# Routed attention in a six-layer decoder: keys and values by blocks of one head, with scatter and gather

## The chip, the cores and the metric

The kernel runs on one core of one Trainium2 chip. The metric is the time of one execution on the device in microseconds (us); of several runs the median is given. All data are fp32, apart from small helpers.

## The reference

The program is a decoder of six sublayers on x of shape 8 x 256 x 512 (2048 tokens, 16 tiles of 128), each followed by an added residual and a layer norm: differential attention, a long convolution, a mixture of 8 experts, self attention, cross attention, and at last the routed attention that the change is about:

```
gating = softmax(x @ W_gate.T)                # 16 heads
idx    = argmax(gating)                       # one head per token
q, k, v = split(x @ W_qkv.T, 3)               # 512 columns each, 16 heads of 32
k_shared = k of head idx of the token         # one key of 32 for each token
v_shared = v of head idx, times max(gating)
att = softmax(causal(q_h @ k_shared.T / sqrt(32)))
y_h = att @ v_shared                          # for all 16 heads of q
x   = layernorm(x + y)
```

Every token has queries for all 16 heads, but only one key and one value of 32 numbers: those of the head that its gate chose. Of the 1024 columns of k and v, 64 are used for a token.

## The kernel before

One core does the sublayers one after the other. Two of them matter here.

**Cross attention** (`cross_attention`, L1548) goes over four groups of four tiles. For each group it turns x (`transpose`, L161), makes queries, keys and values by seven products instead of eight (`seven_products`, L1517: PE makes a product `ps` in PSUM, VectorE adds it on, L1537), and pushes two batches into a small pipeline of scores (`ps_x`), products (`po_x`) and output (`ps_o`, then the residual L1595 and the layer norm, whose reciprocal root runs on GpSimd, L139 and L140). Its instructions are ordered by the compiler's list scheduler, which may move an instruction ahead of others that are not ready. PSUM has four buffers with tag "mm", shared by the products and the transposes.

**Routed attention** (`routed_attention`, L1642) uses the common loop `causal_attention` (L1097). Here the order on PE, VectorE, ScalarE and GpSimd is the order in which the Python code emits the instructions. There are 32 units: four groups of two batches of four units. A unit u does `maxima` (scores `ps_q`, copied by ScalarE at L1160 to `rows`, masked by GpSimd at L1162, reduced by VectorE to `neg` at L1171), `products` of unit u-6 (`ps_pv` by L1257 and L1267, reciprocal L1275, product L1281), and `weights` of unit u-5 (scores again in `ps_k`, L1214; exponential on ScalarE, L1231; mask and a sum on GpSimd, L1232 and L1242). `ps_q` and `ps_k` share one PSUM tile of four banks.

Between these, `fill` and `need` (L1306, L1328) put in the group's other PE work in small steps. Each piece of work has a cost in us and a slot by which it is due; `pressure` (L1341) works out how much must go into each unit. Steps are in the list `queue`; pieces given with `at(..., "fill", ...)` come when nothing else has been begun. `prepare` (L1646) makes the pieces of a group: four turned tiles (`turned_group`, L197), the gate (`gates`, L1656: `ps_g`, then a softmax and the first maximum on VectorE), four `feature_block`s of queries (L1404, `ps_f`), and for each of four tiles two `token_block`s (L1414, `ps_t`): the keys of all 16 heads (512 columns) and the values of all 16 heads. From each of these 128 x 512 products VectorE picks the token's own head:

```
def chosen(dst, ps, by):                                   # L1673
    sel = ps * (one-hot of the head, broadcast over 32)    # L1676
    dst = sum over the 16 heads of sel                     # L1682
```

The keys are repeated four times (`k4`, L1687), turned (`keys_turned`, `pt_k`, L1692) and stored as `kT`. `finish` (L1726) turns the outputs back (`ps_y`), adds the residual into a `row` buffer (`add_norm_later`, L208; three buffers, each held until the norm in the next unit) and stores the tile.

The routing of tokens into blocks of one expert, which the mixture of experts already does (`router`, L669; `blocks`, L902), scatters rows of x to the DRAM tensor `xs` by indirect DMA on GpSimd, reads blocks of 128 rows of one expert back with SyncE's queue, reads the block's expert number into a register of PE (`values_load`, L915), and uses it to address the weights.

Of the kernel before, what the change touches and what calls it, by code (L numbers as in the profile page):

```python
# [23 lines left out]
P = 128  # L24
# [21 lines left out]
NE = (PH * 2 * P - E * (P - 1) - 1) // P + 1  # L46


@with_exitstack
def decoder_kernel(ctx: ExitStack, tc: tile.TileContext, a: dict, out: bass.AP):  # L50
# [43 lines left out]
    ctx_d = dram.tile([P, KB, B * S], F32, tag="ctx_d", name="ctx_d")  # L94

# [101 lines left out]
    def turned_group(work, pools, g):  # L197

        xT = []

        def step(ti):
            if ti == 0:
                xT.append(work.tile([P, KB, GT], F32, tag="xT", name="xT", bufs=1))
            turned(pools, xT[0][:, :, ti * P : (ti + 1) * P], x[g * TPG + ti])

        return xT, [(0, [(TR, lambda ti=ti: step(ti))]) for ti in range(TPG)]
# [405 lines left out]
    def experts(rt):  # L612
# [480 lines left out]
        return clear_slots, load_experts, load_gu_last, router, blocks, combine, wide  # L1093
# [3 lines left out]
    def causal_attention(name, prepare, finish, upb=KB, gather=None):  # L1097
# [18 lines left out]
        with ExitStack() as st:  # L1116
# [177 lines left out]
            def at(slots, place, f):  # L1294

                if place == "fill":
# [210 lines left out]
    def seven_tokens(work, xT):  # L1507

        (b11, b21), (b12, b22) = quadrants(xT)
        t = work.tile([P, 4, 2, S], F32, tag="ts", name="ts", bufs=1)  # L1510
        nc.vector.tensor_tensor(t[:, 0], b12, b11, ALU.subtract)
        nc.gpsimd.tensor_tensor(t[:, 2], b22, b12, ALU.subtract)
        nc.vector.tensor_tensor(t[:, 1], b22, t[:, 0], ALU.subtract)
        nc.vector.tensor_tensor(t[:, 3], b21, t[:, 1], ALU.subtract)
        return b11, b21, t[:, 1], t[:, 2], t[:, 3], t[:, 0], b22

    def seven_products(work, pools, weights, tokens, dst, token_major=False):  # L1517
# [15 lines left out]
        def part(name):  # L1533
            return work.tile([P, 2, S], F32, tag=name, name=name, bufs=1)

        p1, u2, u3 = part("p1"), part("u2"), part("u3")
# [3 lines left out]
        add(u2, product(2), p1)  # L1540
        add(u3, product(3), u2)
# [6 lines left out]
    def cross_attention(wq, wk, wv, wo):  # L1548
        scale = D**-0.5

        def batch(work, pools, ps_s, n, qT, kT, v, cx, ctxT):
# [34 lines left out]
            def out():  # L1586
                for i in range(2):
# [6 lines left out]
                    r = work.tile([P, D], F32, tag="row", name="res")  # L1594
# [6 lines left out]
        with ExitStack() as st:  # L1601
# [7 lines left out]
            for g in range(NG):  # L1609
# [14 lines left out]
                pipe.flush()  # L1624
                kT = work.tile([P, KB, GT], F32, tag="kT", name="kT", bufs=1)
                k = quadrants(kT)
                seven_products(work, pools, wk7, x7, lambda i, l: k[l][i])
                v = work.tile([P, TPG, D], F32, tag="v", name="v_x", bufs=1)
# [13 lines left out]
    def routed_attention(wqkv, wg):  # L1642

        idx = index_row(const, H1, "idx_h")

        def prepare(work, pools, g, at, here):  # L1646
# [5 lines left out]
            k4 = work.tile([P, TPG, 4, HD1], F32, tag="k4", name="k4")  # L1652
            ind = work.tile([P, TPG, H1], F32, tag="ind", name="ind")
            itop = work.tile([P, TPG, H1], F32, tag="itop", name="itop")

            def gates():  # L1656
                ps = pools.tile([P, TPG, H1], F32, tag="mm", name="ps_g")
                for ti in range(TPG):
                    project(
                        ps[:, ti, :],  # L1660
                        lambda k: xT[0][:, k, ti * P : (ti + 1) * P],
                        lambda k: wg[:, k, :],
                    )
                gate = work.tile([P, TPG, H1], F32, tag="gate", name="gate")
                nc.vector.tensor_copy(gate, ps)
                softmax_small(work, gate, H1)
                top = work.tile([P, TPG], F32, tag="top", name="top")
                first_max(work, gate, H1, idx, top, ind)
                nc.vector.tensor_tensor(
                    itop, ind, top.unsqueeze(2).broadcast_to([P, TPG, H1]), ALU.mult  # L1670
                )

            def chosen(dst, ps, by):  # L1673

                sel = work.tile([P, H1, HD1], F32, tag="sel", name="sel")
                nc.vector.tensor_tensor(  # L1676
                    sel,
                    ps.rearrange("p (h d) -> p h d", d=HD1),
                    by.unsqueeze(2).broadcast_to([P, H1, HD1]),
                    ALU.mult,  # L1680
                )
                nc.vector.tensor_reduce(dst, sel.rearrange("p h d -> p d h"), AX.X, ALU.add)  # L1682

            def key(ti, ps):
                k = k4[:, ti]
                chosen(k[:, 0, :], ps, ind[:, ti, :])
                nc.vector.tensor_copy(k[:, 1:4, :], k[:, 0:1, :].broadcast_to([P, 3, HD1]))  # L1687

            def keys_turned():
                pt = pools.tile([P, TPG, P], F32, tag="mm", name="pt_k")  # L1690
# [6 lines left out]
            xT, need = turned_group(work, pools, g)  # L1697
            need.append((0, [(0.8, gates)]))
            need.append((0, feature_block(pools, qT, xT, wqkv, 0, 0, HD1**-0.5)))
            for ti in range(TPG):  # L1700
                need.append(
                    (0, token_block(pools, xT, wqkv, D, ti, lambda ps, ti=ti: key(ti, ps)))
                )
            for c in range(1, 3):
                need.append((0, feature_block(pools, qT, xT, wqkv, 0, c, HD1**-0.5)))
            need.append((0, [(TR, keys_turned)]))
            for c in range(3, KB):
                need.append((c, feature_block(pools, qT, xT, wqkv, 0, c, HD1**-0.5)))
            for ti in range(TPG):
                need.append(  # L1710
                    (
                        5 + ti // 2 * (4 if g == NG - 1 else 2),
# [142 lines left out]
```

## Time and profile before

| what | us |
|---|---|
| median of 3 runs | 2199.62 (2196.56 to 2202.16) |
| the profiled execution | 2202.62 |
| its span, first to last instruction | 2200.8 |
| cross attention, its weights' sums included | from about 1502 to 1843 |
| routed attention | 1843 to 2200.8 |

The mean granted clock of TensorE in the profiled execution is 0.970. In the profile a row of a group gives the line, the engine, the operation, what it writes and reads, the shape and the count, then the busy time in us, the mean of one in ns, and the idle time of the engine before it with what ended it. Durations of PE matmuls overlap, because they are pipelined: the time that one costs in a full stream is the distance between the starts of two. PEld is the weight load, which runs beside the matmul before it; PEldq and PEq are steps of PE's sequencer.

### The profile page before, as it was taken

The numbers are of one execution on the slowest core, as the hardware profiler recorded it, in microseconds if no ns is written. First come the engines' busy times: TensorE is split into PE (matmuls) and PEld (weight loads), VectorE is DVE, ScalarE is ACT, GpSimd is POOL, SyncE is SP. The second block draws the span as 40 slices with busy tenths as digits, with TensorE's granted clock in tenths as the row PEclk, the third lists the DMA queues.
The fourth block names the chain that finished last, engine by engine and source line by source line (L and its number), as shares of the span: only waits on it lengthen the run. The fifth ranks groups of instructions, "written<-read, shape, count | busy, mean of one in ns | idle before, by whom it ended". The sixth has DMA issues, their size and how long they took to land. (4 is left out here: it accounts for less than half of the span.)

```text
span 2200.8 us, 35612 instructions
## 1 busy us (share of the span) xinstructions
PE 2053.4 (93%) x14904; PEld 1192.7 (54%) x14904; DVE 1272.1 (58%) x1923; ACT 598.9 (27%) x723; POOL 824.4 (37%) x918
## 2 busy tenths in 40 slices
PE   7989899879999999999959999999999999999995
PEld 4545555544453455555524444446877875445543
DVE  4676767758888964222235746466344343476777
ACT  4545545520010013111114333340110110333342
POOL 2566767737556723000033644343000000242343
PEclk9989999989999999999989999999999999999998
DMA  6899801335124144131140201002100100000000
GB/s 221 328 385 382 312 1 45 92 87 198 29 76 164 29 148 149 62 141 61 48 145 29 77 20 58 1 2 96 39 20 20 39 0 1 1 11 11 11 18 33
DMA packets 110032, 197.56 MB, mean 90 GB/s; under 512 B 7088, under 2 KB 30768, under 8 KB 109872
## 3 DMA queue, kind: packets, MB, share of 16 engines
q1 hardware_dynamic: 104752, 178.49, 23.4%
q0 software_dynamic: 5120, 16.78, 2.2%
q8 instruction: 120, 1.97, 0.4%
q14 instruction: 40, 0.33, 0.0%
HBM read 93.54 MB, written 112.20 MB: 93 GB/s over the span
## 5 line engine op out<-in xcount | busy, mean ns | idle before, releaser
L1275 DVE RECIPROCAL rsum<-ps_pv 128x256 f32<-128x256 f32 x128 | 224.4, 1753 | 238.1 <-PE ps_pv L1267 237.9
L171 PE MATMUL ps_y<-kv,wt 128*128 128x512 f32 x640 | 282.6, 600 | 4.4 <-POOL kv L519 3.8
L1231 ACT ACTIVATE pT<-ps_k 128x1536 f32<-128x1536 f32 x128 | 185.7, 1450 | 288.9 <-PE ps_k L1223 286.9
L1171 DVE TENSOR_REDUCE neg<-rows 128x12 f32<-128x1536 f32 x128 | 223.1, 1743 | 50.9 <-POOL rows L1162 50.9
L1160 ACT COPY rows<-ps_q 128x1536 f32<-128x1536 f32 x128 | 184.2, 1439 | 184.0 <-PE ps_q L1151 142.2
L1162 POOL TENSOR_SCALAR_AFFINE_SELECT rows<-rows 128x1024 f32<-128x1024 f32 x128 | 140.1, 1094 | 250.3 <-ACT rows L1160 250.0
L1232 POOL TENSOR_SCALAR_AFFINE_SELECT pT<-pT 128x1024 f32<-128x1024 f32 x128 | 141.1, 1102 | 242.9 <-ACT pT L1231 242.9
L171 PEld LDWEIGHTS ps_y<-kv,wt 128*128 128x128 f32 x640 | 120.9, 192 | 154.4 <-issue 135.8
L1242 POOL TENSOR_TENSOR pT<-pT 128x512 f32<-128x512 f32 x112 | 145.2, 1296 | 9.3
L1077 POOL DMA_INDIRECT w_l1x<-ys,slots x32 | 32.9, 1028 | 267.1 <-DMA ys<-y_m 259.2
L182 PE MATMUL ps_t<-w_l1f,xT 128*128 128x512 f32 x256 | 122.0, 611 | 0.0
L182 PE MATMUL ps_f<-xT,w_l1a 128*128 128x512 f32 x256 | 118.2, 604 | 2.9 <-ACT xT L195 2.9
L992 PE MATMUL po_m<-dn,hT 128*128 (+1 forms) x216 | 101.9, 609 | 1.5
L139 POOL TENSOR_SCALAR rstd<-bn_mv 128x1 f32<-128x1 f32 x80 | 16.9, 212 | 217.0 <-DVE bn_mv L145 211.2
L1267 PE MATMUL ps_pv<-pT,ones_v 128*32 128x256 f32 (+1 forms) x1152 | 85.0, 377 | 6.7 <-POOL pT L1242 6.3
L557 DVE TENSOR_REDUCE yc<-z 128x64 f32<-128x512 f32 x128 | 86.0, 673 | 6.2 <-POOL w_l1a L558 5.8
L1151 PE MATMUL ps_q<-kz,qT 32*128 32x128 f32 x1536 | 62.9, 294 | 22.6 <-ACT pT L1231 17.5
L1151 PEld LDWEIGHTS ps_q<-kT,qT 32*128 32x128 f32 x1536 | 49.9, 190 | 56.2 <-issue 17.0
L1151 PEld LDWEIGHTS ps_q<-kz,qT 32*128 32x128 f32 x1536 | 50.4, 192 | 54.8 <-ACT pT L1231 34.4
L182 PEld LDWEIGHTS ps_f<-xT,w_l1a 128*128 128x128 f32 x256 | 46.3, 189 | 54.8 <-issue 49.3
L1151 PE MATMUL ps_q<-kT,qT 32*128 32x128 f32 x1536 | 62.4, 292 | 12.5 <-ACT kT L1411 4.8
L974 DVE TENSOR_TENSOR h_b<-h_b,pg 128x352 f32<-128x352 f32 x36 | 18.8, 521 | 95.3 <-ACT h_b L973 95.3
(326 smaller groups left out, 3744.6 us busy)
## 6 DMA issues: line engine op xcount, KB each, us to landing
xs<-zero SPq DMA_DIRECT2D x8, 4352.0 KB, 31.3
ys<-zero SPq DMA_DIRECT2D x8, 4352.0 KB, 31.4
filters<-in_L_xattn_k SPq DMA_DIRECT2D x4, 2560.0 KB
first_h<-xs SPq DMA_DIRECT2D x36, 256.0 KB, 2.6
ys<-y_m SPq DMA_DIRECT2D x36, 256.0 KB, 2.0
gu<-in_L_ffn_gate_up_proj SPq DMA_DIRECT2D x3, 2816.0 KB, 19.8
wt<-filters SPq DMA_DIRECT2D x32, 256.0 KB, 2.8
x<-in_x SPq DMA_DIRECT2D x16, 256.0 KB, 4.9
```

The lines of the kernel that those rows point to most:

```text
L171: nc.tensor.matmul(ps, lhsT=lhsT(k), rhs=rhs(k), start=(k == 0), stop=(k == n - 1))
L182: nc.tensor.matmul(ps[0], lhsT=lhsT(k), rhs=rhs(k), start=(k == 0), stop=(k == KB - 1))
L557: nc.vector.tensor_reduce(yc[:, lb], z, AX.X, ALU.add)
L992: nc.tensor.matmul(po, lhsT=hT[:m, i, :], rhs=dn[i][:m, bass.ds(e, 1), :], start=(i == 0), stop=(i == len(FCH) - 1),)
L1151: nc.tensor.matmul(block[:, s, j, :], lhsT=q(rows, c, b * S + i * P, P), rhs=k(rows, c, b * S + keys * P, P), start=True, stop=True,)
L1160: nc.scalar.copy(d.rearrange("p j s k -> p s j k"), block)
L1162: nc.gpsimd.affine_select(out=rows, in_=rows, compare_op=ALU.is_ge, fill=-FAR, base=0, pattern=[[0, 8], [-1, P]], channel_multiplier=1,)
L1171: return lambda: nc.vector.tensor_reduce(neg[u // upb % 2][:, :, :, c], d, AX.X, ALU.max, negate=True)
L1231: nc.scalar.activation(p[:, 0:3].rearrange("p j s q -> p s j q"), block, AF.Exp)
L1232: nc.gpsimd.affine_select(out=p[:, 0:2].rearrange("p j s q -> p (j s) q"), in_=p[:, 0:2].rearrange("p j s q -> p (j s) q"), compare_op=ALU ...
L1242: nc.gpsimd.tensor_tensor(p[:, 3], p[:, 1], p[:, 2], ALU.add)
L1275: nc.vector.reciprocal(r, ps[:, 1, :])
```

## The change

Keys and values are no longer made for all heads. Each half of the tokens (8 tiles, 1024 tokens) is gated, its tokens are given places in blocks of 128 rows of one head, and their rows of x are scattered to `xs`. NKB = 8 + 16 - 1 = 23 blocks hold every possible division of 1024 tokens among 16 heads. Each block is loaded, turned by four transposes and multiplied with the 64 columns of its head (32 of the key, 32 of the value) by four matmuls whose weights are addressed by a register. Eight blocks share one PSUM tile (`ps_kv`), which is copied out and stored to a DRAM tensor `kv_d` with rows of 64 numbers; each tile then gathers its tokens' rows by indirect DMA.

The first half is done inside the cross attention: tiles 0 to 3 are turned and gated in group 1, tiles 4 to 7 in group 2, where `choose`, `places` and `send` follow; the blocks are in group 3, eleven before the keys' products and twelve behind them, and then the gathers. The second half is done in the routed attention: its tiles are turned early, in group 0, and kept (`xT2`, `xT3`), then gated; the choice is in unit 4, the places in unit 5, two scatters in each of units 6 to 9, the blocks in four pieces put into the queue at unit 10 and due by units 11 to 14, the gathers at the ends of units 14 and 15. The keys of groups 2 and 3 are turned in the unit before the group.

To make room in SBUF, `seven_tokens` writes one difference over `b12`, `seven_products` puts `u3` into the buffer of `p1`, and the residual rows of the cross attention have three buffers, shared with the blocks' rows.

```diff
+NKB = PH + H1 - 1
+    kv_d = [dram.tile([NKB * P, 2 * HD1], F32, tag=f"kv{i}", name=f"kv{i}") for i in range(2)]
...
-                if place == "fill":
+                if place == "due":
+                    at(slots, "start", lambda: insort(queue, f, key=lambda piece: piece[0]))
+                elif place == "fill":
...
-        nc.gpsimd.tensor_tensor(t[:, 2], b22, b12, ALU.subtract)
+        nc.gpsimd.tensor_tensor(b12, b22, b12, ALU.subtract)
...
+                if g == NG - 1:
+                    steps = half.blocks(work, pools, evacuate)
+                    for f in steps[: NKB // 2]:
+                        f()
                 kT = work.tile([P, KB, GT], F32, tag="kT", name="kT", bufs=1)
                 k = quadrants(kT)
                 seven_products(work, pools, wk7, x7, lambda i, l: k[l][i])
+                if 0 < g < NG - 1:
+                    for ti in range(TPG):
+                        xt = work.tile([P, KB, P], F32, tag="xT_b", name="xT_g")
+                        transpose(pools, xt, x[(g - 1) * TPG + ti], "mm")
+                        half.gate(pools, (g - 1) * TPG + ti, lambda k: xt[:, k, :])
+                if g == NG - 2:
+                    half.choose()
+                    half.places(pools)
+                    half.send(range(PH))
+                if g == NG - 1:
+                    for f in steps[NKB // 2 :]:
+                        f()
+                    for t in range(PH):
+                        half.gather(t)
...
+        def blocks(self, work, pools, copy):
+            xb, xT, out = {}, {}, []
+            def load(b):
+                if b < NKB:
+                    xb[b] = work.tile([P, D], F32, tag="row", name="xb_h", bufs=3)
+                    nc.sync.dma_start(out=xb[b], in_=xs[b * P : (b + 1) * P, :])
+            def turn(b):
+                if b < NKB:
+                    pt = pools.tile([P, KB, P], F32, tag="mm", name="pt_h")
+                    for k in range(KB):
+                        nc.tensor.transpose(pt[:, k, :], xb[b][:, k * P : (k + 1) * P], ident)
+                    xT[b] = work.tile([P, KB, P], F32, tag="xT_b", name="xT_h")
+                    copy(xT[b], pt)
+                    del xb[b]
+                    load(b + 3)
+            def step(b):
+                if b == 0:
+                    for i in range(3):
+                        load(i)
+                    turn(0)
+                turn(b + 1)
+                e = nc.values_load(
+                    self.heads[0:1, b : b + 1],
+                    engines=(mybir.EngineType.PE,),
...
+                if b % 8 == 0:
+                    out.append(pools.tile([P, 8, 2, HD1], F32, tag="mm", name="ps_kv"))
+                xT_b = xT.pop(b)
+                for k in range(KB):
+                    nc.tensor.matmul(
+                        out[-1][:, b % 8],
+                        lhsT=xT_b[:, k, :],
+                        rhs=self.w[:, k, bass.ds(e, 1)],
+                        start=(k == 0),
+                        stop=(k == KB - 1),
+                    )
+                n = b % 8 + 1
+                if n == 8 or b == NKB - 1:
+                    y = work.tile([P, 8, 2 * HD1], F32, tag="sc", name="kv_b")
+                    copy(y[:, :n], out.pop()[:, :n].rearrange("p b a d -> p b (a d)"))
+                    rows = self.rows[(b + 1 - n) * P : (b + 1) * P, :]
+                    nc.sync.dma_start(out=rows.rearrange("(b p) c -> p b c", p=P), in_=y[:, :n])
...
-            for ti in range(TPG):
-                need.append(
-                    (0, token_block(pools, xT, wqkv, D, ti, lambda ps, ti=ti: key(ti, ps)))
-                )
...
+            keys = [(TR, keys_turned)]
+            if g < 2:
+                need.append((0, keys))
+            else:
+                at(2 * KB * g - 1 - here, "due", (2 * KB * g, keys))
...
-            for ti in range(TPG):
-                need.append(
-                    (
-                        5 + ti // 2 * (4 if g == NG - 1 else 2),
-                        token_block(
-                            pools, xT, wqkv, 2 * D, ti,
...
+            if g == 0:
+                other = halves[1]
+                for n in range(2, NG):
+                    late[n], turns = turned_group(work, pools, n, f"xT{n}")
...
+                        need.append((n + ti // 2, steps + [(0.2, gate)]))
+                at(4, "mid", other.choose)
+                at(5, "fill", [(0.4, lambda: other.places(pools))])
+                for i in range(PH):
+                    at(6 + i // 2, ("mid", "end")[i % 2], lambda i=i: other.send([i]))
+                steps = other.blocks(work, pools, nc.scalar.copy)
+                for i in range(4):
+                    piece = [(1.0, f) for f in steps[NKB * i // 4 : NKB * (i + 1) // 4]]
+                    at(10, "due", (11 + i, piece))
+                for i in range(PH):
+                    at(14 + i // TPG, "end", lambda i=i: other.gather(PH + i))
```

`gate` is four matmuls of 16 columns for a tile and a copy to `logits`. `choose` is a softmax and a first maximum of 128 x 128 numbers, and the running counts per head tile by tile; `places` is three matmuls and some sixteen VectorE operations that give each token its slot and each block its head. `send` is one scatter of 128 rows of 2 KB for a tile, `gather` one gather of 128 rows of 256 B, both indirect DMAs issued by GpSimd.

## The prediction

> **What bounds the kernel now.** I read the busy table of the page first: TensorE (PE) is busy for 93% of the span, no other engine for more than 58%. Then I cut the span into stages. The change touches two: the cross attention (1510 to 1842 us) and the routed attention (1843 us to the end). The second I cut again at ScalarE's copies of the scores (L1160 in its timeline), which mark the 32 units of the loop: unit 0 at 1876.0, unit 8 at 1943.5, 16 at 2026.7, 24 at 2112.1, the last (31) at 2155.3. Columns: stretch, length, then busy us of PE, PE weight loads, VectorE (DVE), ScalarE (ACT), GpSimd (POOL), granted clock, DMA share, GB/s.
>
> ```profile
> 1510.00:1842.00 332.00, 327.04 (x1425) 260.18 (x1423) 129.42 (x222) 34.49 (x73) 25.35 (x41) 0.99 0.08 26
> 1843.00:1876.00 33.00, 31.50 (x121) 16.59 (x122) 10.88 (x27) 4.58 (x9) 0.00 (x0) 0.95 0.00 1
> 1876.00:1943.50 67.50, 64.28 (x469) 33.40 (x470) 39.38 (x56) 21.23 (x23) 15.81 (x14) 0.97 0.00 1
> 1943.50:2026.70 83.20, 81.45 (x757) 43.65 (x758) 58.95 (x84) 28.70 (x28) 30.88 (x32) 0.96 0.04 14
> 2026.70:2112.10 85.40, 81.51 (x757) 43.29 (x758) 61.06 (x84) 28.77 (x29) 30.60 (x32) 0.96 0.04 14
> 2112.10:2155.30 43.20, 41.91 (x571) 22.45 (x572) 35.36 (x41) 21.34 (x18) 24.38 (x25) 1.00 0.04 14
> 2155.30:2200.80 45.50, 23.76 (x374) 14.29 (x374) 33.72 (x49) 10.50 (x8) 16.15 (x22) 0.80 0.10 36
> ```
>
> PE is full in every stretch but the last. So PE work taken out of the routed stage shortens it until another engine is met, and PE work put into the cross attention, where PE has 5 idle us of 332, lengthens it by itself. The groups of instructions of the routed stage (1842 to the end, shapes kept apart) say what that work is:
>
> ```profile
> L182 PE MATMUL ps_t<-w_l1f,xT 128*128 128x512 f32 x256 | 122.0, 611 | 0.0
> L182 PE MATMUL ps_f<-xT,w_l1f 128*128 128x512 f32 x128 | 68.4, 671 | 0.0
> L1275 DVE RECIPROCAL rsum<-ps_pv 128x256 f32<-128x256 f32 x32 | 56.0, 1751 | 33.5 <-PE ps_pv L1267 33.3
> L1171 DVE TENSOR_REDUCE neg<-rows 128x12 f32<-128x1536 f32 x32 | 55.8, 1742 | 12.5 <-POOL rows L1162 12.5
> L1682 DVE TENSOR_REDUCE v_r<-sel 128x32 f32<-128x512 f32 x16 | 16.7, 1046 | 0.6
> ```
>
> The first row is keys and values of all heads: 256 instructions, two for each matmul of fp32. Their durations overlap; back to back they start every 0.43 us (16 of L182 in 7.0 us of PE's timeline), so 110 us of PE. This is what the change removes, with VectorE's picks (L1676, L1682, L1687: 59 us), which lie beside PE.
>
> **What one block costs.** A block of 128 rows has 4 transposes (0.11 us each, as pt_k: 4 in 0.44) and 4 products of 64 columns, so 8 instructions. The nearest row is the gate, 16 columns wide: 32 instructions in 3.58 us, 0.112 each. Its pace is that of the weight load, so 64 columns pay the same: 8 x 0.112 = 0.90, with the transposes 1.34 us. Here the Trainium skill (TensorE: Matmul & The Clock Gate, "Back-to-back issue gap") speaks otherwise: a stream of pairs at 128 columns keeps about 81 ns each, which would make the block 12 x 0.081 = 0.97 us and the 46 blocks 17 us cheaper. The same page ("LDWEIGHTS") puts a weight load at its columns divided by 1.2 in ns, 107 for 128, whatever is streamed. The transposes and gates of this trace stand at 0.108 and 0.112, so I take the second. Sixteen times fewer columns are thus only four times less PE time.
>
> Each block also reads its head into a register of PE and makes addresses from it. The expert blocks do the same:
>
> ```profile
> L915 PEldq TENSOR_LOAD <-i_ex x36: 297/302/786, 792.5 to 1094.7; - x36
> ...
> L171 PEldq FUSED_REGOPS  x8: 46/50/60, 1028.2 to 1029.2; - x8
> ```
>
> 0.30 us for the load (least/median/most in ns), and eight address steps in about 1.0 us; four here, so about 0.9 us of PE's sequencer per block, against 1.34 us of array. In the expert blocks (1000 to 1012 us of the timeline, transposes at 1001.73 and 1010.10) the period is 8.37 us, and their matmuls by starts make 8.10: 16 of 0.297, 6 of 0.43, 7 transposes of 0.11. So 0.27 us shows. Bounds for the new block: 0 (hidden in PE's queue) to 0.9 (all shown). I take 0.27, the row, though it lay under longer matmuls: 1.6 us a block.
>
> **The cross attention gains work.** Eight tiles turned again and gated: 8 x (0.44 + 0.90) = 10.7 us. The three matmuls of the places: 0.5. 23 blocks: 37. These add in full. Beside PE: the choice and the places, about 36 small VectorE operations of 0.2 to 0.5 us (the gate's own are 0.22), some 10 us where VectorE is busy 129 of 332; eight scatters on POOL, 1.27 us apart as the expert ones start, then eight gathers, where POOL is busy 25 of 332. Behind the scatters wait the reciprocal roots of later norms, which nothing needs for 20 us. SP's loads of rows take 2.6 us to land (first_h<-xs, 256 KB); three buffers and, with issue and transposes, some 4 us a round give 1.3 us a block, under the 1.6; behind them SP holds only output stores. What could show is PSUM evacuation late behind VectorE's chain, or a load met too early: 0 to 12 us; the products' evacuations now have 1.03 us of slack in 1.73, so I take 3. The reuse of b12, p1 and the third row buffer costs nothing: POOL's difference starts 0.8 us later and is wanted by the fourth product, 5 us in. Sum: +51 us (42 with 1.34 us a block and no stall, 75 with 2.24 and 12).
>
> The Trainium skill (DMA: Bandwidth & Descriptors, "Specifications") speaks against rows of 256 B: under 512 B a transfer loses line rate. The trace has no such transfer near; 1.5 MB are written and 0.5 MB gathered in such rows, with DMA under a tenth busy. The first half's lie tens of us before their use; the second half's gathers come one unit, some 6 us, before it. If such rows took twice the 3.6 us of the trace's gathers (w_l1x<-ys) it would show 1 to 2 us; I take 1, below.
>
> **The routed stage, stretch by stretch.** PE of a unit by starts: 0.88 (ps_q), 1.22 (ps_pv), 1.04 (ps_k) = 3.14 us. A feature block is 3.45.
>
> - Lead, 33 us: keep the last transposes, one feature block (3.45), keys turned (0.44) and copied (0.6), waits 1: 7.
> - Units 0 to 8, 67.5 us: 8 x 0.88 and the first products 5.6 = 12.6; three feature blocks 10.4; turns and gates of the second half 8 x 1.34 = 10.7; the next group's turns, feature block and keys 6.2; 4 unhidden (0.6 waits per unit) and 2 for ACT, which holds its copies while it waits for the choice before its exponential (up to 4.8 us at a gate before): 46.
> - Units 8 to 16, 83.2 us: 8 x 3.14 and small parts 27.4; four feature blocks 13.8; 23 blocks 37; and waits. PE follows the written order here, so: the first rows' load after the last scatter 4 (2.7 and 2.6 less other work); the block's copy behind ACT's 1.45-us exponential, four units, 5.6; gathers 1 (they wait in POOL's order for the last store, with the next unit's masks and so PE's products behind them; the 16 indirect transfers take 20 us of a POOL busy 31 of 83). Then the row buffers: the three slots are shared with the residual rows of a finished pair of tiles, which hold two for about a unit, and one slot left means a load (2.6) and more per block, so 0 to 16, I take 8. Sum 97.
> - Units 16 to 24, 85.4 us: PE 8 x 3.14 + 13.9 + 4 = 43. VectorE: 1.75 + 1.74 + 0.43 a unit, and per four units a split (1.65) and two norms (4.3): 5.4 us, 43 too. Light units ran 6.1 apart before (2033.2, 2039.3, 2045.5). I take 5.9: 47.
> - Units 24 to 31, 43.2 us: four values' picks fewer (1.73 each) on a VectorE busy 35 of 43, but the same PE units: 40.
> - Tail: 45.5, less one pick: 45.
>
> Sum 7 + 46 + 97 + 47 + 40 + 45 = 282 against 357.8: -76. With the +51: **-25 us**. The profiled execution took 2202.6 us, its span 2200.8; the median of the runs is 2199.6, 3 lower, so I take the difference from that: 2175 us.
>
> **Rivals.**
> *Blocks at the pace of their latency (slower than before).* If each block waits in turn for transposes 0.44, copy and its signals 0.9, register work 0.9 and products 0.9, it costs 3.1 us, in both stages: 46 x 1.5 = +70, 2245 us. It decides from 1.6 + 25/46 = 2.1 us a block. For it: PE takes its work in written order in the second half, two turned tiles and three rows are all that is ahead, and register steps have only 0.9-us products to hide under. Against: each step turns the next block before its own products, and in the cross attention products of 1.73 us stand between. Chance 0.22.
> *All of it hidden.* Blocks at 1.34 (-12), no evacuation wait (-3), half the waits of units 8 to 16 (-10), no latency at 0 to 8 (-5): 2145 us. Chance 0.18.
> *The unit loop meets its own floor.* Without fill, scores and weights share four PSUM banks: 0.88, ACT 1.44, 1.04, ACT 1.45 and signals make 5.2 us, VectorE 5.4; if the two interfere, units from 16 on cost 7 and not 5.8: +18, 2193 us, so much of the removed work buys nothing. Chance 0.08.
> *As summed:* 2155 to 2192, most likely 2175. Chance 0.52.
>
> **Numbers.** About 0.3% (6.6 us) is what a measurement of this kernel can tell from no change. Faster 0.72 (as summed, all hidden, a little of the floor); same 0.06 (the floor, and blocks near 2.1 us); slower 0.22. The range 2138 to 2212 takes in all but the upper part of the slow rival and the lower edge of the hidden one.
>
> **What would show it.** The rows ps_t<-w_l1f gone; in the cross stretch PE near full and 51 us longer, ps_kv pairs 0.112 apart; starts of pt_h near 1.6 us apart (at 2.1 or more the slow rival is right); first score copy 7 us after the last norm; units 16 to 24 in 47 us. I am wrong if PE's waits name xb_h loads, xT_h copies or TENSOR_LOAD for more than 25 us together.

## The result, and the profile after

The change makes the kernel slower: 2231.5 us (median of 4 runs, 2225.14 to 2233.45) beside 2200.48 us for the kernel before in the same comparison (4 runs, 2196.56 to 2202.16). The ratio is 1.0133, with a 95% interval of 1.0114 to 1.0152. The prediction was 2175 us, and its range ended at 2212.

The profiled execution took 2225.14 us, its span is 2223.3. Up to the end of the self attention the new profile happens to be 7.3 us ahead of the old one (its last score copy is at 1455.1, not at 1462.4), although the change touches nothing there. So I count from that copy: 738.4 us before, 768.2 after, +29.8. The lengths of stages here and below come from one profile of each kernel. The cross attention before, from that copy (stretch, length, busy us of PE, weight loads, DVE, ACT, POOL, granted clock, DMA share, GB/s):

```profile
1462.40:1843.00 380.60, 371.44 (x1852) 283.66 (x1850) 167.19 (x273) 46.63 (x84) 46.60 (x66) 0.99 0.09 31
```

The stages of the kernel after, cut as those of before, in the same columns: cross attention from that copy, lead, units 0 to 8, 8 to 16, 16 to 24, 24 to 31, tail.

```profile
1455.10:1890.10 435.00, 420.86 (x2230) 331.58 (x2228) 187.04 (x332) 56.92 (x102) 62.83 (x87) 0.98 0.16 48
1890.10:1899.60 9.50, 6.06 (x41) 3.20 (x42) 0.52 (x4) 3.77 (x8) 0.00 (x0) 1.00 0.01 2
1899.60:1969.00 69.40, 58.81 (x486) 38.33 (x490) 30.26 (x61) 26.77 (x32) 17.97 (x17) 0.80 0.03 13
1969.00:2080.50 111.50, 91.21 (x917) 69.12 (x917) 47.13 (x60) 40.73 (x49) 42.11 (x44) 0.80 0.28 84
2080.50:2134.40 53.90, 49.71 (x651) 26.43 (x652) 41.30 (x48) 27.51 (x25) 33.30 (x35) 0.97 0.04 14
2134.40:2177.70 43.30, 35.90 (x550) 20.20 (x550) 37.13 (x48) 21.84 (x18) 24.42 (x24) 0.92 0.07 26
2177.70:2223.30 45.60, 20.62 (x368) 12.76 (x368) 30.81 (x40) 10.51 (x8) 16.19 (x23) 0.84 0.10 36
```

| stage | before | forecast | after | after less forecast |
|---|---|---|---|---|
| cross | 380.6 | +51 | 435.0 (+54.4) | +3.4 |
| lead | 33.0 | 7 | 9.5 | +2.5 |
| units 0 to 8 | 67.5 | 46 | 69.4 | +23.4 |
| units 8 to 16 | 83.2 | 97 | 111.5 | +14.5 |
| units 16 to 24 | 85.4 | 47 | 53.9 | +6.9 |
| units 24 to 31 | 43.2 | 40 | 43.3 | +3.3 |
| tail | 45.5 | 45 | 45.6 | +0.6 |

The sum of the last column is 55, against a miss of 56 in the medians (-25 forecast, +31 measured). The units 0 to 16 hold 38 of it, and there the clock column stands at 0.80, where before it was 0.97 and 0.96. PE is also no longer full: 58.8 of 69.4 and 91.2 of 111.5. The work itself is what the change says. The groups of the routed stage, 1890 us to the end, shapes kept apart:

```profile
L185 PE MATMUL ps_f<-xT,w_l1f 128*128 128x512 f32 x128 | 69.6, 660 | 0.8 <-ACT xT L198 0.8
L1278 DVE RECIPROCAL rsum<-ps_pv 128x256 f32<-128x256 f32 x32 | 56.0, 1750 | 78.5 <-PE ps_pv L1270 78.4
...
L1804 PE MATMUL ps_kv<-w_l1f,xT_h 128*128 x184 | 31.9, 335 | 1.0 <-ACT xT_h L1783 0.6 <-issue 0.4
...
L1781 PE MATMUL pt_h<-ident,xb_h 128*128 128x128 f32 x92 | 19.0, 343 | 14.3 <-DMA xb_h<-xs 14.3
```

The row of 256 products of 512 columns is gone, and so are VectorE's picks. In their place stand 23 blocks of 8 products (184) and 4 transposes (92). But VectorE's reciprocal, which waited 33.5 us for PE before, now waits 78.5, and the transposes of the blocks carry 14.3 us of PE idle time, all of it until a load of rows (`xb_h<-xs`) landed.

Three things go wrong, and the timeline shows each. The first blocks of the second half on PE (start, duration, line, operation, count; in brackets the idle time before it and what ended it):

```profile
1993.33 1.09 PE L1781 MATMUL pt_h<-ident,xb_h 128*128 128x128 f32 x4 [2.78 <-DMA xb_h<-xs]
1994.21 1.81 PE L1804 MATMUL ps_kv<-w_l1f,xT_h 128*128 x8
1997.07 1.09 PE L1781 MATMUL pt_h<-ident,xb_h 128*128 128x128 f32 x4 [1.05 <-DMA xb_h<-xs]
1997.95 1.81 PE L1804 MATMUL ps_kv<-w_l1f,xT_h 128*128 x8
```

The transposes start 3.74 us apart, and for their rows PE waits 2.78 and 1.05 us. SyncE's queue, which issues those loads, tells why (waiting engine and line, what for, total, times, longest):

```profile
...
SPq L1775 <- PE pt_h L1781: 27.2, 18, 3.8
SPq L1775 <- DMA xb_h<-xs: 18.5, 8, 3.0
SPq L1775 <- DVE x L157: 6.7, 2, 5.8
```

The issues wait for the transposes of the block before (18 times), for an earlier load to land (8 times) and for the layer norm's `x` (L157, twice, up to 5.8 us): two of the three `row` slots hold residual rows until that norm. So one slot is left, by this reading, and load and transpose take turns; e1_rows below tests it.

The second thing is in the durations. Eight products of a block take 1.81 us above. In the cross attention the same eight take first 1.81 and then 1.00:

```profile
1777.05 0.63 PE L1781 MATMUL pt_h<-ident,xb_h 128*128 128x128 f32 x4 [2.13 <-DMA xb_h<-xs]
1778.80 2.28 PE L1804 MATMUL ps_kv<-w_l1f,xT_h 128*128 x10 [1.12 <-DVE xT_h L120]
...
1790.25 1.06 PE L1781 MATMUL pt_h<-ident,xb_h 128*128 128x128 f32 x4
1791.11 1.81 PE L1804 MATMUL ps_kv<-w_l1f,xT_h 128*128 x8
1792.71 1.06 PE L1781 MATMUL pt_h<-ident,xb_h 128*128 128x128 f32 x4
...
1796.83 0.61 PE L1781 MATMUL pt_h<-ident,xb_h 128*128 128x128 f32 x4
1797.28 1.00 PE L1804 MATMUL ps_kv<-w_l1f,xT_h 128*128 x8
1798.12 0.61 PE L1781 MATMUL pt_h<-ident,xb_h 128*128 128x128 f32 x4
```

The transposes start 2.46 us apart up to 1796 and 1.29 us apart behind it, with no waits in brackets in either part: PE works at half speed. The clock column of the two stretches says the same:

```profile
1780.00:1796.00 16.00, 16.00 (x81) 16.00 (x81) 2.07 (x3) 1.75 (x3) 0.00 (x0) 0.50 0.41 124
1796.00:1830.00 34.00, 33.65 (x245) 31.19 (x244) 10.57 (x16) 5.85 (x10) 0.00 (x0) 1.00 0.41 110
```

Granted clock 0.50 for 16 us in which PE is busy all 16, then 1.00. Ahead of it lie the wait of 2.13 us for the first blocks' rows and one of 1.12 us for a copy. From the first of the blocks to unit 16 the granted clock is halved from 1778.9 (17.1 us), 1912.0 (3.4), 1922.3 (20.5), 1949.6 (3.4), 1990.5 (30.7), 2028.1 (10.2) and 2075.9 (3.4). From the first score copy of unit 0 to that of unit 16 that makes 71.6 us, and PE is busy in 59.1 of them; before it was 10.2 us (3.4 at 1909.3 and 6.8 at 1987.8, behind and among the gates of a group).

The third is in units 1 to 3, eight times over: turn a tile, wait for its copy, gate it. One of them in PE's timeline:

```profile
1922.95 1.09 PE L197 MATMUL pt<-ident,x 128*128 128x128 f32 x4
1924.72 1.89 PE L174 MATMUL ps_g<-w_l1f,xT 128*128 128x16 f32 x8 [0.68 <-ACT xT L198]
```

Each gate waits 0.67 to 1.00 us for ScalarE's copy of the tile just turned, and the eight instructions of a gate take 1.89 us where the clock is halved (1.06 or 1.07 in the first three gates) rather than the 0.9 that I had summed.

### The profile page after: what moved, and what is told of

It is laid out like the page before. It is cut to its first block, busy times and chain, and to the rows that moved or that the text cites. A ratio compares the mean times of both kernels' runs of the same rounds, so it can differ in the third digit from the quotient of the medians.

```text
span 2223.3 us, 36817 instructions
## 1 busy us (share of the span) xinstructions
PE 2033.4 (91%) x15244; PEld 1235.3 (56%) x15244; DVE 1239.7 (56%) x1900; ACT 625.1 (28%) x768; POOL 855.8 (38%) x954
## 5 line engine op out<-in xcount | busy, mean ns | idle before, releaser
L1174 DVE TENSOR_REDUCE neg<-rows 128x12 f32<-128x1536 f32 x128 | 223.0, 1742 | 49.4 <-POOL rows L1165 49.4
L1154 PE MATMUL ps_q<-kT,qT 32*128 32x128 f32 x1536 | 66.7, 307 | 17.0 <-ACT pT L1234 10.2
L1154 PEld LDWEIGHTS ps_q<-kz,qT 32*128 32x128 f32 x1536 | 51.0, 194 | 54.6 <-ACT pT L1234 34.3
L1217 PE MATMUL ps_k<-qT,kT 32*128 32x256 f32 (+1 forms) x1024 | 69.1, 357 | 4.6 <-ACT rows L1163 2.8
## 6 DMA issues: line engine op xcount, KB each, us to landing
ys<-zero SPq DMA_DIRECT2D x8, 4352.0 KB, 31.9
```

The costliest lines, as they stand in the source:

```text
L1154: nc.tensor.matmul(block[:, s, j, :], lhsT=q(rows, c, b * S + i * P, P), rhs=k(rows, c, b * S + keys * P, P), start=True, stop=True,)
L1174: return lambda: nc.vector.tensor_reduce(neg[u // upb % 2][:, :, :, c], d, AX.X, ALU.max, negate=True)
L1217: nc.tensor.matmul(block[:, s, at, :], lhsT=k(rows, c, b * S + j * P, P), rhs=q(rows, c, b * S + j * P, P * (2 - j)), start=True, stop=False,)
```

## The experiments

Four theories. **Row slots:** the second half's blocks crawl because residual rows hold two of three slots. **Turn and gate:** the waits between a tile's turn and its gate cost most of what is missed in units 0 to 8. **Clock:** what costs most is not the waits but the halved clock that follows them and outlasts them. **Thin streams:** PE loses its clock even without a wait where only transposes and products of 16 columns run. The rival to all of them is that the change, once its waits are gone, still doesn't pay: its work in the cross attention is as dear as what it saves.

The kernel before took 2212 us on the chip of the first four runs and 2217 on that of the last three, so ratios are compared, and stages by their lengths.

**e1_rows: own slots for the second half's rows.** The blocks of the routed stage get three buffers of their own; the cross attention is unchanged.

```diff
-                    xb[b] = work.tile([P, D], F32, tag="row", name="xb_h", bufs=3)
+                    xb[b] = work.tile([P, D], F32, tag=row[0], name="xb_h", bufs=row[1])
...
-                steps = other.blocks(work, pools, nc.scalar.copy)
+                steps = other.blocks(work, pools, nc.scalar.copy, ("row_h", 3))
```

> The second half's blocks get three row buffers of their own; everything else is as in the changed kernel. Theory 1 (row buffers: the residual rows hold two of three shared slots for a unit, so each block waits for its own load): the blocks of units 10 and 11 start some 2 us apart and not 3.9, the stretch of 44 us from the first block to the middle of unit 12 shrinks by about 16 us, and TensorE's half clock there goes with it, 5 us more: about 2210 us. Rival (each block is slow by its own latency, register and copy): the pace stays, within 5 us of 2231.

Measured: 2225.03 us (9 runs), ratio 1.0064 (1.0033 to 1.0095), half of the loss gone: 15 us by the ratios, where I had expected 21. Its units 8 to 16, and in them the stretch of the first blocks (columns as above):

```profile
1983.90:2076.90 93.00, 80.39 (x918) 57.86 (x918) 47.14 (x60) 40.56 (x50) 44.32 (x46) 0.94 0.34 102
2005.00:2028.00 23.00, 19.32 (x205) 16.79 (x205) 8.42 (x13) 9.81 (x15) 6.50 (x9) 1.00 0.59 174
```

Two of these blocks in PE's timeline:

```profile
2007.51 0.60 PE L1781 MATMUL pt_h<-ident,xb_h 128*128 128x128 f32 x4
2007.95 1.00 PE L1804 MATMUL ps_kv<-w_l1f,xT_h 128*128 x8
2008.79 0.61 PE L1781 MATMUL pt_h<-ident,xb_h 128*128 128x128 f32 x4
```

Blocks 1.28 us apart where they had been 3.9, the clock at 1.00 in their stretch, and the stage at 93.0 in place of 111.5: -18.5 us. The row slots are shown. The 18.5 us are of two kinds: PE's idle time fell from 20.3 to 12.6 us, and its busy time for the same instructions from 91.2 to 80.4. So 7.7 us were waits. The 10.8 us of busy time go with the clock that came with the waits: its half time in this stage fell from 44.3 to 10.2 us.

**e2_gates: each gate two turned tiles behind its turn.** The order of emission alone.

```diff
-                        need.append((n + ti // 2, steps + [(0.2, gate)]))
+                        behind.append((0.2, gate))
+                        last = behind if t == NT - 1 else behind[:1] if len(behind) > 2 else []
+                        need.append((n + ti // 2, steps + last))
+                        behind = behind[len(last) :]
```

> In group 0 of the routed attention each gate of the second half comes two turned tiles behind its own, so that PE need not wait for ScalarE's copy. Theory 2 (eight waits of 0.7 us for the copy, and the half clock that they bring from 1912 to 1950 us): 5 us of waits and about 8 us of slow clock are saved, 2218 us, with the granted clock near 1.0 in units 2 to 4. Rival (these units are full of PE work that the sum missed): under 4 us saved, clock as before.

Measured: 2238.35 us (4 runs), ratio 1.0118 (1.0093 to 1.0143), which can't be told from the change itself (I had expected 13 us less). Units 0 to 8 fall from 69.4 to 62.0. The waits are gone, but not the half clock. Two gates in PE's timeline, on both sides of 1930.7:

```profile
1928.47 1.01 PE L174 MATMUL ps_g<-w_l1f,xT 128*128 128x16 f32 x8
...
1935.70 1.73 PE L174 MATMUL ps_g<-w_l1f,xT 128*128 128x16 f32 x8
```

The two stretches by their busy times and clock:

```profile
1925.40:1930.70 5.30, 5.30 (x49) 5.22 (x47) 0.52 (x3) 2.83 (x5) 0.07 (x1) 1.00 0.00 0
1930.70:1944.40 13.70, 13.34 (x97) 12.75 (x97) 5.16 (x13) 3.90 (x4) 1.09 (x1) 0.50 0.00 1
```

For 5.3 us PE is busy without a gap at full clock, with transposes and gates only; then the clock is 0.50 for 13.7 us, with PE busy 13.3 of them and no wait above 0.36 us. So moving the gates gains 7.4 us, 5.0 of them PE's idle time, and the stage still runs 16 us over the forecast. What the stage gained was lost in units 8 to 16 (119.7 for 111.5, with 54.6 us at half clock among the blocks); why the clock was worse there, no run tells.

**e3_warm: spare products where the blocks wait.** 23 products of 128 x 512 are put ahead of the transposes of early blocks and thrown away (5 in the cross attention, 18 in the routed stage), some 20 us of PE work by the 0.86 us of such a product.

```diff
                     pt = pools.tile([P, KB, P], F32, tag="mm", name="pt_h")
+                    spare = {1: 3, 2: 2} if self.first == 0 else {1: 2, 2: 2, 3: 2, 4: 2, 5: 2, 6: 2, 7: 2, 8: 2, 9: 2}
+                    for _ in range(spare.get(b, 0)):
+                        nc.tensor.matmul(
+                            pt.rearrange("p k q -> p (k q)"), lhsT=ident, rhs=self.wide, start=True, stop=True
+                        )
```

> Spare products of 128 x 512, thrown away, stand ahead of the turned rows at which PE waits: five in the cross attention (blocks 1 and 2), two each at blocks 1 to 9 of the second half; 23 in all, 20 us of PE work more. Theory 3 (half the block time is TensorE's clock, halved after PE has idled): the blocks after it in the cross attention start 1.3 us apart and not 2.45, 5 to 8 us saved there, the blocks of units 12 and 13 likewise, and the kernel is faster in spite of the added work, about 2220 us. Rival (the clock follows something else, or waits alone matter): slower by the part of the 20 us that no wait covers, 2235 to 2250 us.

Measured: 2233.05 us (4 runs), ratio 1.0094 (1.0071 to 1.0118). Not slower than the change, with 20 us more work on the engine that bounds it. By the ratios it is 9 us faster, where I had expected 11, but the two intervals still touch. The first blocks of the cross attention, then the two whole stages (cross attention, units 8 to 16):

```profile
1787.80:1806.00 18.20, 17.47 (x125) 14.12 (x124) 6.18 (x10) 3.52 (x6) 0.94 (x3) 1.00 0.52 156
1468.90:1898.10 429.20, 417.22 (x2240) 324.75 (x2238) 187.00 (x332) 57.05 (x102) 62.88 (x87) 1.00 0.16 49
1979.20:2087.20 108.00, 96.93 (x954) 63.38 (x954) 47.27 (x60) 40.91 (x49) 44.40 (x47) 0.95 0.30 88
```

The cross attention took 429.2 us in place of 435.0 although 4.3 us of products were added, and nearly all of its blocks start 1.3 to 1.4 us apart. Units 8 to 16 took 108.0, against 111.5, with 15.5 us added. If only the waits mattered, the spare products could hardly have done better than cost nothing. But take them out of PE's busy time, and the rest of its work took 81.4 us in units 8 to 16 (91.2 in the change) and 412.9 in the cross attention (420.9). So the clock is a cost of its own, and filling waits with useless work paid for itself here.

**e4_half0: the first half alone.** Tiles 0 to 7 by blocks, groups 2 and 3 as before.

```diff
+            if g in (2, 3):
+                xT, need = turned_group(work, pools, g)
...
+                            token_block(
+                                pools, xT, wqkv, 2 * D, ti,
+                                lambda ps, ti=ti: chosen(v[:, ti, :], ps, itop[:, ti, :]),
+                            ),
...
+                return views(need)
-            if g == 0:
+            if False:
```

> The first half alone by blocks of one head (its work in the cross attention, as in the changed kernel); groups 2 and 3 of the routed attention make keys and values of all heads as before. If the loss lies in the second half's blocks inside the ordered unit loop: the cross attention stays 54 us longer, lead and units 0 to 16 take about 118 us and not 184, the rest as before: about 2187 us, faster than before. Rival (the work put into the cross attention is what doesn't pay): over 2200 us.

Measured: 2215.72 us (20 runs), ratio 1.0018 (1.0002 to 1.0034): within 0.2% of the kernel before, where I had expected a gain. Lead and units 0 to 16 take 134.3 us in place of 183.7 (-49.4), and the cross attention 432.9 in place of 380.6 (+52.3). That is the rival's answer for the first half. The second half therefore makes nearly all of the loss of the change: units 16 to 24 save 31.9 (85.8 to 53.9), and units 0 to 16 pay 21.8 (47.6 to 69.4) and 34.3 (77.2 to 111.5), 24 us more than they get. The routed stage, with PE and granted clock in units 0 to 8 and 8 to 16:

```profile
1912.80:1960.40 47.60, 39.10 (x381) 21.28 (x382) 19.90 (x19) 22.36 (x23) 14.60 (x14) 0.89 0.00 1
1960.40:2037.60 77.20, 73.26 (x738) 40.39 (x742) 54.54 (x83) 29.19 (x29) 31.95 (x33) 0.93 0.04 15
```

Turning and gating eight tiles was summed at 10.7 us, with 2 for waits; 21.8 is what the second half's eight, with their choice and places, add to units 0 to 8.

**e6_wide: gates that stream 128 columns.** As e2_gates, but each product of the gate streams 128 columns of the weights' tile, of which 112 are thrown away.

```diff
-            ps = pools.tile([P, H1], F32, tag="mm", name="ps_g")
-            project(ps, xT, lambda k: self.wg[:, k, :])
...
+            ps = pools.tile([P, P], F32, tag="mm", name="ps_g")
+            end = 3 * D * KB + H1
+            project(ps, xT, lambda k: w_slot[:, end + k * H1 - P : end + k * H1])
```

> As the kernel with the gates two tiles behind, but each gate streams 128 columns and keeps the last 16 (the other 112, of other weights, are thrown away); at 0.11 us an instruction, the pace of the weight load, this costs no time by itself. That kernel's units 0 to 8 took 61.9 us, and TensorE ran at half clock for 13.7 us in the middle of a run of turned tiles and gates without a wait longer than 0.4 us. Theory 4 (a stream of 16-column products does too little to hold the clock): with wide gates the half clock in units 2 to 4 goes or shrinks below 7 us, units 0 to 8 take about 55 us. Rival (the clock falls for the waits before and after): the same half clock, units 0 to 8 within 2 us of 62.

Measured: 2241.61 us (4 runs), ratio 1.0130 (1.0076 to 1.0184). The stretch behaves as the theory says, the whole gains nothing:

```profile
1937.24 0.60 PE L197 MATMUL pt<-ident,x 128*128 128x128 f32 x4
1937.68 1.06 PE L174 MATMUL ps_g<-w_l1f,xT 128*128 128x128 f32 x8
```

Eight times the columns at the same pace (the eight gate instructions take 1.06 us, those of 16 columns 1.01), and in units 0 to 8 no half clock before 1951.7. The Trainium skill (TensorE: Matmul & The Clock Gate, "Part 4: PE-mode transpose") says of transposes that they don't count as PE being busy in the way that products do, which would explain why this mix is at risk at all; no run here leaves the transposes out. They are the same in both kernels: what differs is the columns of the products between them. Units 0 to 8 take 56.4 us, e2_gates 62.0, and the whole difference is PE's busy time (50.6 for 56.4). The cross attention, where the gates stream 128 columns too, had 20.5 us at half clock among its blocks here and 10.2 in e2_gates, and took 5.1 us longer, which takes back most of what the routed gates gave. So thin streams as a cause are shown in units 0 to 8 only, by one profile of each kernel.

**e7_half0x: the first half, its rows loaded early.** As e4_half0, with the rows of its blocks in the memory of the cross attention's query weights, which are done with by then: four buffers, loaded before the pipeline is emptied.

```diff
                 if g == NG - 1:
+                    free = [wq[:, k, :] for k in range(KB)]
+                    begin_loads, steps = half.blocks(work, pools, evacuate, ("", KB, free))
+                    begin_loads()
```

> The first half alone by blocks, as before, but the rows of its blocks go to four buffers in the memory of the query weights, which are free by then, so that they are loaded beside the outputs' products ahead of the first block. Theory 1 with 3 (the first block's wait for its load, and the half clock after it, are what the cross attention pays beside the work itself): no half clock in the blocks, the cross attention 10 us shorter than the 433 it took, and the whole 5 us faster than before, ratio about 0.998. Rival (the cross attention is longer by its work alone): 430 us or more, ratio 1.002 as without it.

Measured: 2208.09 us (10 runs), ratio 0.9970 (0.9948 to 0.9992), a little faster than the kernel before, as expected. The cross attention:

```profile
1464.50:1888.00 423.50, 412.03 (x2230) 322.70 (x2228) 186.87 (x332) 57.10 (x102) 63.00 (x87) 1.00 0.16 50
```

423.5 us at a clock of 1.00, in place of 432.9 in e4_half0: -9.4. With the first rows there in time PE never waits for them, and among the blocks the clock is never halved.

**e8_all: both halves, with what was learnt.** Rows of the first half as in e7_half0x; six own buffers for the second half, loaded a unit ahead; scatters four to a unit, blocks from unit 9, gathers from 13; and turns and gates put between steps of feature blocks.

```diff
+                    f, n = features[c], len(small) // 2
+                    need.append((c + 1, f[:1] + small[:n] + f[1:3] + small[n:] + f[3:]))
...
-                    at(6 + i // 2, ("mid", "end")[i % 2], lambda i=i: other.send([i]))
-                steps = other.blocks(work, pools, nc.scalar.copy)
+                    at(6 + i // 4, ("mid", "end")[i % 2], lambda i=i: other.send([i]))
+                begin_loads, steps = other.blocks(work, pools, nc.scalar.copy, ("row_h", 6))
+                at(8, "end", begin_loads)
```

> The changed kernel with all that the experiments point to: rows in the memory of the query weights (first half) and in six buffers of their own (second half), loaded a unit ahead; scatters four a unit; the second half's blocks, loads and gathers one unit earlier; turned tiles and gates between the steps of the feature blocks. If the waits and the half clock that they bring were the loss, and not the work: cross attention 422, lead 9.5, units 0 to 8 52 us, 8 to 16 85, 16 to 24 51, 24 to 31 43.5, tail 46, in all some 25 us faster than before, ratio 0.988. Rival (the work of 46 blocks eats the gain wherever it stands, and the waits come back elsewhere): ratio 0.998 or more.

Measured: 2205.71 us (10 runs), ratio 0.9960 (0.9937 to 0.9983): faster than before, by less than expected. Its cross attention, units 0 to 8 and units 8 to 16:

```profile
1468.20:1891.60 423.40, 412.28 (x2230) 322.89 (x2228) 186.86 (x332) 57.09 (x102) 62.96 (x87) 1.00 0.16 50
1902.80:1961.80 59.00, 51.80 (x482) 33.88 (x482) 32.74 (x61) 27.06 (x32) 18.51 (x17) 0.88 0.05 19
1961.80:2057.00 95.20, 80.11 (x921) 56.58 (x921) 44.46 (x58) 40.97 (x51) 43.77 (x45) 0.97 0.32 97
```

What PE waited for longest in the last two:

```profile
PE pt_k L1858 <- ACT k L1851: 6.4, 2, 4.0
PE ps_pv L1260 <- POOL pT L1235: 5.1, 1, 5.1
```

From the last score copy of the self attention to the end it takes 730.8 us (before 738.4, the change 768.2). One new wait is mine: POOL's mask waits behind the scatters, which now come four to a unit (5.1 us). The keys' transposes wait twice for ScalarE's copy (6.4 us), as they did in the change (5.8). Even so the same work runs 37 us shorter than in the change. How the gain divides between the edits of this kernel isn't measured, apart from the two told above (9.4 and 18.5).

What keeps it from more is to be seen in PE's busy time. From the last score copy to the end PE is busy for 657.3 us here and for 695.8 before: 38.6 us of its work are gone, but only 7.6 us of time. PE's idle time grew from 42.6 to 73.5 us (85.0 in the change).

## Why the prediction was wrong

**The step that failed** is one that all of the sums rest on and that is nowhere in them: each PE duration was taken from rows at full clock, and no term stood for the clock. The prediction sums "8 x 1.34" for turned and gated tiles and "23 blocks 37" wherever they run. Its terms for units 0 to 16 hold 118 us of PE work and 25 us of waits. The profile has 150.0 us busy and 30.9 idle: 32 of the 38 us missed are busy time of PE, and only 6 are waits. In the same stages the time at half clock grew from 10.2 to 71.6 us. PE was busy for 59.1 of them, so by itself the half clock accounts for up to 30 us.

What lowers the clock, by these runs, is how PE was filled just before; what brings it back stays open. With its waits taken away (e1_rows) or filled (e3_warm), the same work of units 8 to 16 took 10.8 and 9.8 us less of PE's time; with wider products in the gates (e6_wide), that of units 0 to 8 took 5.8 less. It was to be seen before the change: each of the four gates there has 3.4 to 6.8 us at half clock in it or just behind it, though 512-column products surround it, and the stage of 83.2 us has 0.96 in its clock column, not 1.00. The change takes the 512-column products away and puts small ones behind waits.

The Trainium skill (TensorE: Matmul & The Clock Gate, "HAM oscillation — how this bites in real kernels") describes a pattern like this: waits for loads between short bursts of products make PE fall to half speed, so that each burst starts cold. The waits that it tells of are longer than its window of 3.4 us ("What's actually happening"). Here the halved lengths are mostly multiples of 3.4 us, but the clock fell at 1778.9 behind waits of 2.13 and 1.12 us, and in e2_gates behind 5.3 us without a gap. The way back differs too. By the section on the window one busy window restores the clock; here PE was busy for 16.00 of 16.00 us at 0.50. An estimate from the page, one window at half clock for each fall, would lose 1.7 us a fall; the runs show up to 30.7 us at half clock in one piece.

**Units 0 to 8,** 69.4 for 46, can be taken apart with e4_half0, which has all but the second half's work there and takes 47.6. For that rest I had 33.3 (46 less 10.7 and 2). Of the 14.3 between, 3.4 are a feature block too few in my sum (41 instructions in that trace, 32 counted; eight make a block), up to 5 are 10.2 us of half clock, and 4.6 are waits (8.6 for 4: queries, keys, a score copy, the split of the maxima). The remaining 1 to 2 us may be that the block's instructions run in pairs between other work; that is not measured. The second half's turns and gates cost 21.8 for 12.7: PE's busy time grew by 19.7 where I had 10.7, its idle time by 2.1 where I had 2. Of the 9 us more busy time up to 7 are half clock, and 1.3 the products of the places, which I had left out here.

**The row slots:** "0 to 16, I take 8": 18.5 (e1_rows). As a wait the term was right, 7.7 us; what it lacked is the clock, 10.8 us, that those waits brought down. What is left of units 8 to 16 then stands at 93.0 for 89 (97 less the 8), right in its sum only. A block costs 0.3 us less than I took, some 7 us for 23, and as much is lost elsewhere. One part is known: the keys' transposes waited 5.05 us at 2069.9 (4.28 in the change, at 2075.5) for ScalarE's copy of gathered keys, where I allowed 1. Another is 10.2 us at half clock.

**Units 16 to 24,** 53.9 for 47: VectorE, which I took for the limit at 43, is busy 41.3; PE is busy 49.7. Again the trace has 39 instructions of feature blocks where I counted 32 (3 us), 3.4 us of half clock (up to 1.7), and pairs that keep PE for 1.05 us from start to next start (2110.96 to 2112.01) where 0.86 was taken from a block in one piece; some 16 of them would make 3. That these two stages were given one block too few each is a plain error of mine. These parts are my estimates; no run takes them one by one.

**What was right.** The lead (7; 9.5), units 24 to 31 and the tail within 3 us. The cross attention in its sum, +51 against +54.4, but not in its terms: a block costs 1.28 to 1.30 us at full clock, not 1.6, so the register work hides fully, and an instruction costs 0.107 us, the pace that the prediction chose over 0.081. 23 of them are 30, and with 10.7 and 0.5 that makes 41; the undisturbed cross attentions of e7_half0x and e8_all stand at +42.9. The other 11.5 us are late rows and half clock (2.7 us of idle and 8.8 of busy time more than in e7_half0x), which the 7 us too much for registers and the 3 for stalls covered by luck.

**A comparison that misleads** is "sixteen times fewer columns are thus only four times less PE time". It sets one block against one tile: 16 products of 0.43 us are 6.9, five times 1.34. But 46 blocks stand for 16 tiles, so by the prediction's own figures 110 us become 62, and not even half is saved. The sums themselves count 46 blocks, rightly.

**The rivals.** The slow one had the sign, and what I had named as its mark came true (starts of `pt_h` 2.1 us apart or more), but its mechanism did not: the first ten blocks of the second half came 3.4 to 5.6 us apart through slots and clock, not through their own chain, which runs at 1.28 once rows and clock are there. My alarm ("more than 25 us together") did not sound: PE's waits for `xb_h`, `xT_h` and registers come to 18 us in the profile after. A halved clock is in no list of waits; it makes busy time longer. The rule "PE work taken out shortens it until another engine is met" failed as well: in e8_all 38.6 us of PE's work are gone for 7.6 us of time, and another engine is near full only in units 24 to 31 (VectorE, 39.1 of 42.5 us). That the change pays only undisturbed is what e7_half0x and e8_all show, and then by 0.3 to 0.4%, since +43 us in the cross attention stand against what the routed stage gives back.

## What to carry to other kernels

Before pricing work that replaces long products with short ones, look at the granted clock around the short ones that are already there, and price the new ones at half speed, as an upper bound, wherever a wait or a thin stream comes first. To tell waits from clock between two runs, compare PE's idle time and its busy time apart. When a buffer is shared, count how many slots are free at the moment of use, and charge load and use in turn if it is one. A saving on the bounding engine is worth its time only if what is left keeps that engine full.

## What the hardware showed that I had not expected

- The granted clock stays at 0.50 through long stretches in which PE is busy: 16.00 of 16.00 us (change, 1780 to 1796) and 13.34 of 13.70 (e2_gates). At 1796 it came back in the midst of the same blocks, with nothing in PE's instructions that differs. With spare products of 512 columns put in (e3_warm), or with the rows there in time (e7_half0x: 14.1 us of transposes and 64-column products alone), it held at 1.00 all through them. So the same stream ran on at either clock.
- Transposes and products of 16 columns, without a gap, lost the clock after 5.3 us (e2_gates); with 128 columns at the same pace, and score products among them, they didn't in 13 us; there the clock fell at 1951.7, behind a wait of 2.17 us (e6_wide). The number of columns streamed seems to count, not the busy share; two profiles show it, and no run varies the width of the gates further.
- A register load of 0.30 us (46 of them in the change) and the address steps of a block cost nothing that shows behind 1.28 us of PE work.
- The same code fell for different times: the cross attentions of the change, e1_rows, e2_gates and e4_half0 have the same PE instructions and 17.1, 20.5, 10.2 and 10.2 us at half clock among their blocks, and took 435.0, 437.2, 432.4 and 432.9 us.
